# Layer 1 of a two-layer transformer block, worked in two halves of the tokens

## The chip, the cores and the metric

The kernel runs on one core of one Trainium2 chip. The metric is the device time of one execution in microseconds, the median of several runs. The engines are TensorE (PE, with its weight loads listed apart as PEld), VectorE (DVE), ScalarE (ACT), GpSimd (POOL) and SyncE (SP), which issues most of the transfers. Each engine runs its own queue of instructions in order, and engines wait for one another by semaphores.

## The reference

Two transformer layers over 1024 tokens of width 512, all in fp32. Each layer has six modulation vectors, `mod = silu(c) @ wmod`: shift, scale and gate for the attention and for the feed-forward. Cut to what matters here:

```python
for l in range(2):
    sa, ca, ga, sb, cb, gb = mod[l]          # each of width 512
    ga, gb = sign(ga) * max(|ga|, 0.25), sign(gb) * max(|gb|, 0.25)
    x = x + ga * attn[l](layernorm(x) * (1 + ca) + sa)
    x = ... ffn[l](layernorm(x) * (1 + cb) + sb) ...

# layer 0: attention, 32 heads of 128, 8 key heads, causal, 4-bit weights;
#          feed-forward silu(gate) * up -> down, hidden width 1376, each with a LoRA term of rank 16
# layer 1 attention: qkv = h @ w_qkv.T + b_qkv; 32 heads of 16, 8 key heads (each shared by 4)
#          rope on interleaved pairs; causal softmax; out @ w_o.T + b_o
# layer 1 feed-forward: base = h @ base_W.T
#          logits = h @ gate_W.T (28 experts), top 2, softmax of the two
#          lora = sum_e gate_e * 2 * (h @ A_e.T) @ B_e.T, rank 8 each
#          out = x + gb * (base + lora)
```

Layer 1's queries of tokens 0 to 511 need only keys of tokens 0 to 511. Those of 512 to 1023 need all keys.

## The kernel before

Tokens lie on the 128 partitions in 8 tiles; `x[t]` stays in SBUF from start to end. A matmul with a 512-wide fp32 right side appears as two records of about 0.43 us. A product over the width 512 is four matmuls over chunks `c` of 128, with the transposed activations `hT` (features on partitions) as weights.

**Helpers.** `mod_column` (L121) gets a shift or scale by a DVE product and sum over a streamed piece of `wmod` (L127). `mod_gate` (L133) gets a gate vector, replicated over all partitions, by four matmuls (L140), each with a streamed 256 KB piece `wm` (L139). `layernorm_mod` (L153) does statistics on DVE (L160, L161), a square root on ACT (L163), the normalized `xn` (L168), transposes on PE (L176) and the scaled and shifted `hT` on DVE (L184) or ACT (L179). `evict` (L74) takes PSUM to SBUF on DVE or ACT in turn.

**Order.** The code lists the work in order; a tile framework puts in the semaphores and may move an instruction a little ahead or back on its engine. [...] Pools of tiles are opened and closed by stage, and a new stage's tile waits until the old owner of its place has been read for the last time.

1. Layer 0 attention (L196 to L440), untouched but for helpers.
2. Layer 0 feed-forward (L442 to L536). The LoRA terms are merged into the weights by small matmuls and DVE adds (`merge_gate_up` L476, `merge_down` L488). For each of 11 hidden blocks `j` and each half `b` of the tokens, gate and up products (L510), a sigmoid on ACT and two DVE products. Then the down projection: for each of 8 token tiles eleven 512-wide matmuls (L530), the gate (L535) and the add to `x` (L536).
3. Preparation of layer 1's attention (L539 to L648): loads, layernorm of all 8 tiles, modulation chunks 2 to 5, the output bias times its gate added to `x` on POOL (L587), and then in each token tile `t` the qkv product (L606, widths 512 and 256), the bias (L610), rope over separate even and odd elements shared by DVE and POOL (L627, L633, L634), 16 transposes (L646) of queries and of keys repeated four times, and their eviction to `qT1` and `kT1`.
4. Layer 1 attention (L649 to L845) in 16 units of 512 queries (half `Q`) and one key head `g` (four query heads). A unit has three parts: `maxima_steps` (scores of queries on partitions, L682, with row maxima on DVE, L687 and L694), whose result is written into a spare row of the queries (`maxima_rows`, L709 to L714); `probs_steps` (scores again with keys on partitions, L726, a causal mask L733, exp on ACT L737); and `context` (L749), with a copy (L758) and `normalize` (L760). These score matmuls use 32 rows of the array. The maxima of unit n+2 run between the probability steps of unit n; `later(n, fn)` and `tick` place the other parts so many steps behind. After the last unit of a half, `finish_half` transposes the context (L779, L781) and multiplies it by `w_o` (L787, L791, L792). Score tiles take turns in three pairs of PSUM banks; one bank serves contexts and products ("mm"), one transposes ("tr").
5. Layer 1 feed-forward (L847 to L939): loads, layernorm, logits and LoRA-A products (L873), the top-2 routing in small DVE instructions over all 8 tiles (L880 to L913), and in each tile a gated hidden (L917), two transposes (L925, L926), two ACT copies (L928, L929), four base matmuls (L933), two LoRA-B matmuls (L934, L935), the gate (L937), the residual (L938), and the transfer out (L939).

Of the kernel before, what the change touches and what calls it, by code (L numbers as in the profile page):

```python
# [16 lines left out]
P = 128  # L17
# [24 lines left out]
def block_kernel(ctx: ExitStack, tc: tile.TileContext, a: dict, out: bass.AP):  # L42
# [90 lines left out]
    def mod_gate(l, j):  # L133

        rep = mod[l, "rep"]
        ps = psum_mm()
        for k in range(NC):
            wm = tmps["w"].tile([P, D], F32, tag="ws", name="wm")
            nc.sync.dma_start(wm, a[f"wmod{l}"][bass.ts(k, P), bass.ts(j, D)])  # L139
            nc.tensor.matmul(ps, lhsT=rep[:, k, :], rhs=wm, start=(k == 0), stop=(k == NC - 1))  # L140
        sgn = tmp("sgn")
        nc.vector.tensor_scalar(sgn, ps, 0.0, 2.0, ALU.is_ge, ALU.mult)
        nc.vector.tensor_scalar(sgn, sgn, -1.0, None, ALU.add)
        mag = tmp("mag")
        nc.vector.tensor_mul(mag, ps, sgn)
        g = const.tile([P, D], F32, tag=f"gate{j}", name=f"gate{j}")
        nc.vector.scalar_tensor_tensor(g, mag, 0.25, sgn, ALU.max, ALU.mult)
        mod[l, j] = g
# [293 lines left out]
    with ExitStack() as st:  # L442
        hp = st.enter_context(tc.tile_pool(name="f0h", bufs=1))
        wk = st.enter_context(tc.tile_pool(name="f0k", bufs=3))
        tmp_open(st, "f0", wm=4)
        psum_open(st, "psF0")
        sp = st.enter_context(tc.tile_pool(name="f0s", bufs=2, space=PSUM))
# [6 lines left out]
        gu = hp.tile([P, NF, 2, NC, P], F32, tag="gu", name="gu")  # L454
# [8 lines left out]
        dw = hp.tile([P, NF, D], F32, tag="dw", name="dw")  # L463
        for j in range(NF):
            nc.gpsimd.dma_start(dw[:, j, :], a["d_w"][bass.ts(j, P), :])
# [19 lines left out]
        def merge_down(j):  # L485
# [5 lines left out]
            nc.vector.tensor_tensor(dw[:, j, :], dw[:, j, :], ps, ALU.add)  # L491

        mod_prepare(1)
        mod_chunk(1, 0)
        mod_chunk(1, 1)
        hT = layernorm_mod(hp, mod[0, 3], mod[0, 4])
# [4 lines left out]
        hid = []  # L501
        for j in range(NF):
            hj = hp.tile([P, S], F32, tag=f"hid{j}", name=f"hid{j}")
            hid.append(hj)
            for b in range(2):
                pgu = []
                for m in range(2):
                    ps = sp.tile([P, 512], F32, tag=f"gu{m}", name=f"pgu{m}")
                    for c in range(NC):
                        nc.tensor.matmul(  # L510
                            ps, lhsT=gu[:, j, m, c, :], rhs=hT[b][:, c, :],
# [6 lines left out]
                nc.vector.tensor_mul(hj[:, bass.ts(b, 512)], pgu[1], sg)  # L518
# [5 lines left out]

        for b in range(2):
            for i in range(4):
                t = 4 * b + i
                ps = psum_mm()
                for j in range(NF):
                    nc.tensor.matmul(  # L530
                        ps, lhsT=hid[j][:, bass.ts(t, P)], rhs=dw[:, j, :],
                        start=(j == 0), stop=(j == NF - 1),
                    )
                o = tmp("fo")
                nc.vector.tensor_mul(o, ps, mod[0, 5])  # L535
                nc.vector.tensor_add(x[t], x[t], o)  # L536


    with ExitStack() as st:  # L539
        hp = st.enter_context(tc.tile_pool(name="a1h", bufs=1))  # L540
        prep = st.enter_context(ExitStack())
        SC1 = 1.0 / math.sqrt(HD1)
        NQK = NH + NKV
        HH = HD1 // 2
        MX = HD1


        qT1 = hp.tile([P, NKV, S], F32, tag="qT1", name="qT1")
        kT1 = hp.tile([P, NKV, S], F32, tag="kT1", name="kT1")
        v1 = hp.tile([P, NT, NKV, 32], F32, tag="v1", name="v1")  # L550
        mpad = [hp.tile([P, 4, REP, 32], F32, tag=f"mpad{i}", name=f"mpad{i}") for i in range(2)]
        nc.gpsimd.memset(v1, 0.0)
        nc.gpsimd.memset(v1[:, :, :, MX : MX + 1], 1.0)
        for m in mpad:
            nc.gpsimd.memset(m, 0.0)
        cmaskT = hp.tile([P, P], F32, tag="cmaskT", name="cmaskT")
        nc.gpsimd.memset(cmaskT, 0.0)
        nc.gpsimd.affine_select(
            cmaskT, cmaskT, pattern=[[1, P]], compare_op=ALU.is_ge, fill=NEG, base=0,
            channel_multiplier=-1,  # L560
        )

        cwide = hp.tile([P, 512], F32, tag="cwide", name="cwide")
        nc.gpsimd.memset(cwide[:, : 3 * P], 0.0)
        nc.gpsimd.tensor_copy(cwide[:, 3 * P :], cmask)

        hp = prep.enter_context(tc.tile_pool(name="a1i", bufs=1))
        wk = prep.enter_context(tc.tile_pool(name="a1j", bufs=2))
        tmp_open(prep, "a1", wm=4)
        psum_open(prep, "psP1")  # L570
        wqkv = hp.tile([P, NC, NQKV1], F32, tag="wqkv", name="wqkv")
        for c in range(NC):
            nc.sync.dma_start(wqkv[:, c, :], a["w_qkv"][bass.ts(c, P), :])
        cs = hp.tile([P, NT, 2, HH], F32, tag="cs", name="cs")
        nc.sync.dma_start(cs, a["cs1"])
        bqkv = hp.tile([P, NQKV1], F32, tag="bqkv", name="bqkv")
        nc.sync.dma_start(bqkv, a["b_qkv"].partition_broadcast(P))

        hT = layernorm_mod(hp, mod[1, 0], mod[1, 1])
        for j in (2, 3, 4, 5):  # L580
            mod_chunk(1, j)

        bo = tmp("bo")
        nc.sync.dma_start(bo, a["b_o"].partition_broadcast(P))
        nc.gpsimd.tensor_tensor(bo, bo, mod[1, 2], ALU.mult)
        for t in range(NT):
            nc.gpsimd.tensor_tensor(x[t], x[t], bo, ALU.add)  # L587
# [3 lines left out]
        pads = []  # L591
        for i in range(2):
            qpad = hp.tile([P, NH, 32], F32, tag=f"qpad{i}", name=f"qpad{i}")
            nc.gpsimd.memset(qpad, 0.0)
            pads.append(qpad)
        kpad = hp.tile([P, NKV, REP, 32], F32, tag="kpad", name="kpad")
        nc.gpsimd.memset(kpad, 0.0)
        nc.gpsimd.memset(kpad[:, :, :, MX : MX + 1], 1.0)

        for t in range(NT):  # L600
            qkv = wk.tile([P, NQKV1], F32, tag="qkv", name="qkv")
            for n0 in range(0, NQKV1, 512):
                w = min(512, NQKV1 - n0)
                ps = psum_mm()
                for c in range(NC):
                    nc.tensor.matmul(  # L606
                        ps[:, :w], lhsT=tok(hT, c, t), rhs=wqkv[:, c, n0 : n0 + w],
                        start=(c == 0), stop=(c == NC - 1),
                    )
                nc.vector.tensor_add(qkv[:, n0 : n0 + w], ps[:, :w], bqkv[:, n0 : n0 + w])  # L610
            nc.gpsimd.tensor_copy(
                v1[:, t, :, :HD1],
                qkv[:, NQK * HD1 :].rearrange("p (g e) -> p g e", e=HD1),
            )

            qk = qkv[:, : NQK * HD1].rearrange("p (h i two) -> p h i two", i=HH, two=2)
            cosb = cs[:, t, 0, :].unsqueeze(1).to_broadcast([P, NQK, HH])
            sinb = cs[:, t, 1, :].unsqueeze(1).to_broadcast([P, NQK, HH])
            m = {}
            for name, part, tab, eng in (  # L620
                ("rc", 0, cosb, nc.vector),
                ("is", 1, sinb, nc.gpsimd),
                ("rs", 0, sinb, nc.gpsimd),
                ("ic", 1, cosb, nc.vector),
            ):
                m[name] = wk.tile([P, NQK, HH], F32, tag=f"m{name}", name=f"m{name}", bufs=1)
                eng.tensor_tensor(m[name], qk[:, :, :, part], tab, ALU.mult)  # L627
            qpad = pads[t % 2]
            for half, (u, v, op) in enumerate(
                (("rc", "is", ALU.subtract), ("rs", "ic", ALU.add))  # L630
            ):
                sl = slice(half * HH, (half + 1) * HH)
                nc.vector.tensor_tensor(qpad[:, :, sl], m[u][:, :NH, :], m[v][:, :NH, :], op)  # L633
                nc.gpsimd.tensor_tensor(  # L634
                    kpad[:, :, :, sl],
                    m[u][:, NH:, :].unsqueeze(2).to_broadcast([P, NKV, REP, HH]),
                    m[v][:, NH:, :].unsqueeze(2).to_broadcast([P, NKV, REP, HH]),
                    op,
                )
            qf = qpad.rearrange("p h e -> p (h e)")  # L640
            kf = kpad.rearrange("p g r e -> p (g r e)")
            for src in (qf, kf):
                for g0 in range(0, NKV, 4):
                    ps = psum_tr()
                    for i in range(4):
                        nc.tensor.transpose(ps[:, i, :], src[:, bass.ts(g0 + i, P)], ident)  # L646
                    dst = kT1 if src is kf else qT1
                    evict(dst[:, g0 : g0 + 4, bass.ts(t, P)], ps)  # L648
# [373 lines left out]
```

## Time and profile before

| | |
|---|---|
| median of 3 runs | 2067.97 us (2065.26 to 2074.07) |
| the profiled execution | 2064.12 us, its span 2062.1 us |
| mean granted TensorE clock | 0.961 |
| busy PE / PEld / DVE / ACT / POOL | 1895.3 / 872.4 / 1214.6 / 650.7 / 259.2 us |
| a record of the 512-wide base matmul (L933), mean of the group, ends modelled | 592 ns |
| add of 512 wide from PSUM on DVE (L535) | 0.69 us |
| exp of 128 x 1024 on ACT (L737), in the chain of waits | 1.03 us |
| add of 128 x 512 on POOL (L587) | 1.40 us |
| modulation piece `wm`, 256 KB, issue to landing | 3.5 us |

The page cuts the span into forty slices; a digit is the busy share in tenths, and the clock row is the granted TensorE clock in tenths of full speed:

```profile
PE   5979999999999999999999699998779989989988
PEclk9999999999999999999999799998885889999999
```

Each slice is 51.6 us. Layer 1 begins in slice 27 (counted from 0), and the slices behind it have the lower digits.

### The profile page before, as it was taken

The page shows a single profiled execution, that of the slowest core. Times are in us where ns is not written, and L with a number is a line of the kernel's source. Part 1 is how long each engine was busy: PE and PEld are TensorE (multiplying, and loading weights), DVE is VectorE, ACT ScalarE, POOL GpSimd, SP SyncE. Part 2 cuts the span into 40 slices and gives each one's busy share as a digit, 9 for nine tenths or more (in the row PEclk, how much of TensorE's full clock was granted, in tenths as well). Part 3 has the DMA queues.
Part 4 walks back from the last instruction along what each step waited for, and adds up shares of the span by engine and source line. Part 5 has one row for each costly group of instructions (what it writes and reads, how often), then busy time and mean ns, then how long its engine had stood idle before and what let it go on. Part 6 is the DMA issues. An engine that isn't in the chain of part 4 may idle for free.

```text
span 2062.1 us, 20310 instructions
## 1 busy us (share of the span) xinstructions
PE 1895.3 (92%) x6470; PEld 872.4 (42%) x6470; DVE 1214.6 (59%) x2613; ACT 650.7 (32%) x1174; POOL 259.2 (13%) x233
## 2 busy tenths in 40 slices
PE   5979999999999999999999699998779989989988
PEld 3434454444544445444444344443443333323344
DVE  5666656676566765666755532224566776566433
ACT  2133424434244343343354200000012333344531
POOL 0211111121111211212200100001530000000010
PEclk9999999999999999999999799998885889999999
DMA  5355343444334444343533700002100000000011
GB/s 190 101 117 134 94 115 91 107 122 125 89 109 98 132 110 113 97 107 103 131 88 87 260 14 0 0 0 88 39 21 1 1 1 1 1 1 1 1 40 41
DMA packets 88265, 153.15 MB, mean 74 GB/s; under 512 B 20928, under 2 KB 33856, under 8 KB 88160
## 3 DMA queue, kind: packets, MB, share of 16 engines
q1 hardware_dynamic: 87280, 148.98, 26.6%
q0 software_dynamic: 880, 2.88, 0.4%
q8 instruction: 52, 0.85, 0.2%
q14 instruction: 53, 0.43, 0.1%
HBM read 74.18 MB, written 2.10 MB: 37 GB/s over the span
## 4 chain that ended last, share of the span: by engine, by line
PE 70%; DVE 13%; DMA 6%; ACT 5%; issue 3%; SPq 2%; POOL 1%; DVEq 0%; POOLq 0%; ACTq 0%
PE mm L240 13%; PE mm L370 9%; PE pgu L510 7%; PE sc L326 7%; PE mm L359 7%; PE sc L726 6%; PE mm L530 4%; PE ctx L749 4%; PE sc L682 3%; DMA os<-in_s_o_dram 3%; DVE sm L694 2%; ACT pr L737 2%; SPq L350 2%; PE mm L280 1%; DVE pr L348 1%
## 5 line engine op out<-in xcount | busy, mean ns | idle before, releaser
L336 ACT ACTIVATE pr<-sc,nb 128x1024 f32<-128x1024 f32 (+7 forms) x256 | 187.8, 736 | 374.1 <-DVE nb L333 265.0
L240 PE MATMUL mm<-hT,wf 128*128 128x512 f32 x640 | 283.9, 596 | 6.4 <-ACT wf L257 6.4
L359 PE MATMUL mm<-pT,v 128*128 128x512 f32 x576 | 266.6, 609 | 22.8 <-DMA pT<-pr 22.8
L326 PE MATMUL sc<-kT,qT 128*128 128x512 f32 (+3 forms) x768 | 273.3, 487 | 3.4 <-ACT pr L336 3.4
L370 PE MATMUL mm<-wo,ctxT 128*128 128x512 f32 x512 | 236.1, 599 | 16.8 <-ACT ctxT L365 13.4
L737 ACT ACTIVATE pr<-sc 128x1024 f32<-128x1024 f32 (+1 forms) x192 | 152.8, 810 | 235.5 <-DVE sc L733 169.4
L326 PEld LDWEIGHTS sc<-kT,qT 128*128 128x128 f32 x768 | 139.3, 190 | 153.5 <-issue 127.6
L342 ACT ACTIVATE pr<-pr,rs 128x1024 f32<-128x1024 f32 (+7 forms) x256 | 187.4, 768 | 48.6 <-DVE rs L341 48.4
L726 PE MATMUL sc<-qT,kT 32*128 32x512 f32 (+3 forms) x768 | 179.6, 572 | 22.7 <-ACT pr L737 19.3
L348 DVE STREAM_TRANSPOSE pr<-pr 128x1024 f32<-128x1024 f32 (+7 forms) x256 | 178.1, 747 | 21.3 <-ACT pr L342 16.0
L333 DVE TENSOR_REDUCE nb<-sc 128x1 f32<-128x1024 f32 (+7 forms) x256 | 187.6, 749 | 3.4
L240 PEld LDWEIGHTS mm<-hT,wf 128*128 128x128 f32 x640 | 122.2, 192 | 157.3 <-issue 147.9
L359 PEld LDWEIGHTS mm<-pT,v 128*128 128x128 f32 x576 | 111.1, 196 | 149.6 <-issue 134.8
L682 PE MATMUL sc<-kT,qT 32*128 32x512 f32 (+3 forms) x768 | 159.6, 588 | 14.0 <-ACT pr L737 9.8
L376 POOL TENSOR_TENSOR x<-x,ot 128x512 f32<-128x512 f32 x64 | 81.8, 1278 | 672.3 <-DVE ot L375 568.8
L510 PE MATMUL pgu<-hT,gu 128*128 128x512 f32 x352 | 154.9, 600 | 0.8 <-DVE dw L491 0.8
L370 PEld LDWEIGHTS mm<-wo,ctxT 128*128 128x128 f32 x512 | 94.1, 190 | 132.6 <-issue 94.3
L694 DVE CUSTOM_DVE_ANT_0 sm<-sc,cwide 128x128 f32<-128x128 f32 (+3 forms) x256 | 125.1, 489 | 29.6 <-PE sc L726 8.4
L726 PEld LDWEIGHTS sc<-qT,kT 32*128 32x128 f32 x768 | 60.4, 197 | 139.1 <-ACT pr L737 61.8
L341 DVE RECIPROCAL rs<-rs 128x1 f32<-128x1 f32 x256 | 37.9, 156 | 127.8 <-ACT pr L336 126.4
L250 POOL TENSOR_TENSOR qT<-t,t 128x512 f32<-128x512 f32 x64 | 86.1, 1345 | 180.7 <-DVE t L249 180.7
L510 PEld LDWEIGHTS pgu<-hT,gu 128*128 128x128 f32 x352 | 66.9, 192 | 88.6 <-issue 80.7
(159 smaller groups left out, 1812.5 us busy)
## 6 DMA issues: line engine op xcount, KB each, us to landing
pT<-pr SPq DMA_DIRECT2D x128, 128.0 KB, 2.4
pT<-pr SPq DMA_DIRECT2D x128, 112.0 KB, 2.3
pT<-pr SPq DMA_DIRECT2D x128, 96.0 KB, 2.1
pT<-pr SPq DMA_DIRECT2D x128, 80.0 KB, 2.1
wm<-in_wmodT_dram SPq DMA_DIRECT2D x32, 256.0 KB, 3.5
wi<-in_qw_q_dram SPq DMA_DIRECT2D x32, 256.0 KB, 3.0
ws<-in_s_q_dram SPq DMA_DIRECT2D x32, 256.0 KB, 3.7
oi<-in_qw_o_dram SPq DMA_DIRECT2D x32, 256.0 KB, 2.8
```

The source lines that it names most:

```text
L240: nc.tensor.matmul(ps, lhsT=wf[:, c, :], rhs=hT[half][:, c, :], start=(c == 0), stop=(c == NC - 1),)
L326: nc.tensor.matmul(ps[:, n0 : n0 + w], lhsT=qT[u.g * REP + r][:, bass.ts(u.qi, P)], rhs=kT[u.g][:, n0 : n0 + w], start=True, stop=True,)
L333: nc.vector.tensor_reduce(nb, ps[:, :nk], AX.X, ALU.max, negate=True)
L336: nc.scalar.activation(pr.rearrange("p b k i -> p k b i"), ps[:, :nk].rearrange("p (k b i) -> p k b i", b=NB, i=B), AF.Exp, bias=nb, accum ...
L342: nc.scalar.activation(pr, pr, AF.Copy, scale=rs)
L348: nc.vector.transpose(t, t)
L359: nc.tensor.matmul(ps, lhsT=vv[u.g][:, kj, :], rhs=u.pT[:, :, :, kj, :].rearrange("p a r i -> p r a i"), start=(kj == 0), stop=(kj == u.n ...
L370: nc.tensor.matmul(ps, lhsT=u.ctxT[:, r, :], rhs=wo[u.g][:, r, :], start=(r == 0), stop=(r == REP - 1),)
L510: nc.tensor.matmul(ps, lhsT=gu[:, j, m, c, :], rhs=hT[b][:, c, :], start=(c == 0), stop=(c == NC - 1),)
L682: nc.tensor.matmul(ps[:, j, :w], lhsT=qT1[kp, u.g, bass.ts(qi, P)], rhs=kT1[kp, u.g, n0 : n0 + w], start=True, stop=True,)
L726: nc.tensor.matmul(ps[:, j, :w], lhsT=kT1[kp, u.g, bass.ts(kb, P)], rhs=qT1[kp, u.g, u.Q * QW + q0 : (u.Q + 1) * QW], start=True, stop=True,)
L737: nc.scalar.activation(pr[:, :, :w], ps[:, :, :w], AF.Exp, scale=SC1)
```

## The change

Layer 1 is worked in two halves of 512 tokens. `ln_half` does the layernorm of four tiles, `prep_qkv` and `prep_turn` the preparation of one tile. Those of the first half are listed between the down projections of the second half; those of the second half between the steps of the first attention units; the feed-forward of the first half between the steps of the second half's units, by a list `beside` of pieces, each with the number of step pairs after which it is issued. The second half's feed-forward comes last. Rope is rewritten over tables of full width (cosine repeated, sine with its sign) with all its products on DVE; evictions of preparation go to ACT. Gates and chunks of modulation move: chunk 2's gate behind gate/up block 2, the columns 3 and 4 behind blocks 9 and 10, chunk 5's gate into the attention. The pool "big" lets tiles of the stages take one another's place by tags (gate/up weights, then keys and values; hidden, then queries; down weights, then probabilities; `hT` of layer 0, then of layer 1, then contexts, then `hT` of the feed-forward). The streamed `wm` has two buffers in place of four. All layernorm, qkv, transposes and logits of layer 1 take their PSUM from the same three pairs of banks as the scores; `maxima_rows`, `normalize`, the output projection, the gate of chunk 5 and the feed-forward's turns and outputs share one bank ("tr").

The core of the diff; removed lines that come back indented otherwise, or with only names changed, are left out:

```diff
-    def mod_gate(l, j):
+    def mod_gate(l, j, bank=None):
-        ps = psum_mm()
+        ps = (bank or psum_mm)()
...
-        tmp_open(st, "f0", wm=4)
+    tmp_open(st, "f0", bufs=5, wm=2)
+    dwt = big.tile([P, NF, D], F32, tag="c", name="dw")
...
+    def ln_half(half, shift, scale1, pair):
+        mv = small.tile([P, 4, 2], F32, tag="mv", name="mv")
+        for i in range(4):
+            bs = small.tile([P, 6], F32, tag="bnst", name="bnst")
+            nc.vector.bn_stats(bs, x[4 * half + i])
+            nc.vector.bn_aggr(mv[:, i, :], bs)
+        rstd = small.tile([P, 4], F32, tag="rstd", name="rstd")
+        nc.scalar.activation(rstd, mv[:, :, 1], AF.Sqrt, bias=eps_t)
...
+        h = big.tile([P, NC, 512], F32, tag=f"h{half}", name=f"hT{half}")
+        hTc[half] = h
+        for c0 in range(0, NC, 2):
+            ps = pair()
...
             if j in (0, 1, 4, 5):
                 merge_gate_up(4 if j < 4 else 8, j % 4)
             elif j in (6, 7, 8):
                 for i in range(4 * (j - 6), min(NF, 4 * (j - 5))):
                     merge_down(i)
+            elif j == 2:
+                mod_chunk(1, 2)
+            elif j in (9, 10):
+                mod_chunk(1, j - 6)
...
+    sp = st.enter_context(tc.tile_pool(name="ring", bufs=3, space=PSUM))
...
+    def pair():
+        return sp.tile([P, 2, 512], F32, tag="sc", name="sc")
...
+    def prep_ln(half):
+        ln_half(half, mod[1, 0], mod[1, 1], pair)
+        for i in range(4):
+            t = 4 * half + i
             nc.gpsimd.tensor_tensor(x[t], x[t], bo, ALU.add)
...
+    def prep_qkv(t):
+        qkv = pq.tile([P, NQKV1], F32, tag="qkv", name="qkv")
+        ps = pair()
...
+        nc.vector.tensor_add(qkv, ps.rearrange("p j n -> p (j n)")[:, :NQKV1], bqkv)
+        nc.scalar.copy(
...
+        nc.vector.tensor_tensor(
+            t1, qk, cs[:, t, 0, :].unsqueeze(1).to_broadcast(full), ALU.mult
+        )
+        t2 = pq.tile(full, F32, tag="t2", name="t2")
+        for two in range(2):
+            nc.vector.tensor_tensor(
+                t2[:, :, two::2], qk[:, :, 1 - two :: 2],
+                cs[:, t, 1, two::2].unsqueeze(1).to_broadcast([P, NQK, HD1 // 2]), ALU.mult,
+            )
+        nc.vector.tensor_tensor(qpad[:, :, :HD1], t1[:, :NH, :], t2[:, :NH, :], ALU.add)
+        rep = [P, NKV, REP, HD1]
+        nc.vector.tensor_tensor(
+            kpad[:, :, :, :HD1],
...
+    def prep_turn(t):
...
+            ps = pair()
+            psf = ps.rearrange("p j n -> p (j n)")
+            for g in range(NKV):
+                nc.tensor.transpose(psf[:, bass.ts(g, P)], src[:, bass.ts(g, P)], ident)
+            nc.scalar.copy(dst, psf.rearrange("p (g s) -> p g s", s=P))
+
+    prep_ln(0)
+    for i in range(4):
+        down(4 + i)
+        prep_qkv(i)
+        prep_turn(i)
...
+    def psum_one():
+        return psA[0].tile([P, 512], F32, tag="tr", name="tr")
...
+    def out_transpose(Q, i):
...
+        ps = psum_one()
...
+    def project_out(t, cT):
+        po = psum_one()
...
+    def open_late():
+        prep.close()
...
+        nc.sync.dma_start(wo1, a["w_o"].rearrange("(c p) n -> p c n", p=P))
...
         nc.sync.dma_start(wag, a["e_ag"].rearrange("(c p) n -> p c n", p=P))
...
         nc.sync.dma_start(wb, a["e_base"].rearrange("(c p) n -> p c n", p=P))
...
+    def ffn1_logits(half):
...
+        for i0 in range(0, 4, 2):
+            ps = pair()
...
+    def ffn1_route():
...
+        full = [P, 4, NE]
...
+    def ffn1_turn(t):
...
+        ps = psum_one()
...
+    def ffn1_out(t):
+        hgT, eb = late_pool["hgT", t], late_pool["eb"]
+        po = psum_one()
...
+    def ffn1_pieces(half):
+        yield lambda: ln_half(half, mod[1, 3], mod[1, 4], pair)
+        yield lambda: ffn1_logits(half)
+        yield ffn1_route
+        for i in range(4):
+            yield lambda t=4 * half + i: ffn1_turn(t)
+            yield lambda t=4 * half + i: ffn1_out(t)
...
+    beside = [(2, lambda: prep_ln(1))]
+    for i in range(4):
+        beside.append((4 + 5 * i, lambda t=4 + i: prep_qkv(t)))
+        beside.append((7 + 5 * i, lambda t=4 + i: prep_turn(t)))
+    beside.append((24, open_late))
+    beside.append((25, lambda: mod_gate(1, 5, psum_one)))
+    for i, fn in enumerate(ffn1_pieces(0)):
+        beside.append((48 + 4 * i, fn))
+    count = 0
...
+            count += 1
+            while beside and beside[0][0] <= count:
+                beside.pop(0)[1]()
...
+    for fn in ffn1_pieces(1):
+        fn()
```

A unit of the first half has 4 step pairs and one of the second half 8, so counts 2 to 25 lie in the first seven of the first half's units, and 48 to 88 from the end of the second to the end of the seventh of the second half's.

## Prediction

> **What bounds the kernel now.** I read the busy shares first: PE 1895.3 of 2062.1 us, so only 167 us of the whole span are PE idle, and a change that removes no matmul can win only from that idle time and from time at a low clock. Then I cut the part that the change touches into stages and read the table of stretches:
>
> ```profile
> core 0: us, PE busy (x) PEld busy (x) DVE busy (x) ACT busy (x) POOL busy (x), PEclk, DMA share, GB/s
> 1178.20:1345.50 167.30, 166.53 (x408) 71.11 (x408) 48.17 (x78) 14.42 (x23) 0.00 (x0) 0.99 0.06 23
> 1345.50:1421.20 75.70, 75.54 (x177) 33.09 (x175) 16.80 (x31) 0.30 (x1) 0.05 (x1) 1.00 0.00 0
> 1421.20:1467.90 46.70, 27.35 (x74) 14.55 (x75) 26.75 (x48) 3.30 (x5) 23.05 (x26) 0.75 0.44 139
> 1467.90:1534.00 66.10, 51.24 (x230) 34.90 (x230) 43.24 (x58) 9.38 (x16) 29.75 (x36) 0.95 0.00 0
> 1534.00:1557.00 23.00, 19.03 (x77) 9.31 (x78) 17.50 (x69) 0.25 (x1) 0.00 (x0) 0.56 0.16 47
> 1557.00:1715.00 158.00, 143.87 (x881) 56.16 (x879) 114.46 (x363) 49.35 (x72) 0.00 (x0) 0.81 0.00 1
> 1715.00:1968.00 253.00, 233.56 (x1504) 80.51 (x1504) 144.97 (x348) 115.77 (x142) 5.08 (x4) 1.00 0.00 1
> ...
> 1992.00:2062.10 70.10, 62.76 (x212) 35.02 (x210) 27.48 (x59) 10.88 (x28) 1.27 (x1) 1.00 0.08 30
> ```
>
> In order: gate/up, down projection, the layernorm of layer 1, its eight tiles of preparation, the maxima of two attention units, the eight units of the first half, the eight of the second, and the last feed-forward. Gate/up, down, the second half and the tail are full of PE at full clock. The hole is 1421 to 1534: 112.8 us with 78.6 of PE. The chain of waits says what fills it:
>
> ```profile
> 1434.71 4.95 PE mm L140 x8
> 1439.67 3.33 DMA wm<-in_wmodT_dram
> 1443.76 3.50 DMA wm<-in_wmodT_dram
> 1448.49 3.76 DMA bo<-in_b_o_dram
> 1452.42 1.28 POOL bo L585
> 1453.77 5.98 POOL x L587 x5
> 1459.75 1.03 issue
> 1460.79 3.95 POOL x L587 x3
> 1467.92 1.94 PE tr L646 x8
> ...
> 1480.09 1.74 PE mm L606 x8
> ```
>
> Transfers of the modulation chunks, then POOL's adds of the bias, then in each tile transposes that wait for rope (period 8.8 us, 1486.10 to 1494.90 in the chain).
>
> **Layernorm and half the preparation go beside the down projection.** Before, 1345.5 to 1534 is 188.5 us. Afterwards PE does there: eight down tiles, 75.5; four qkv products, each 3.44 (four 512-wide matmuls, as the chain's "3.44 PE mm L933 x8") plus 1.74 (the row above), 20.7; sixteen transposes a tile, 19.8 us for 128 in the groups of L646, so 2.5, together 10; the layernorm's transposes of one half, half of the 8.1 us of L176's 32, so 4. That is 110. Rope now lies on DVE alone: add 1.1 (L610, twice 557 ns), first product 0.86 (0.69 for 512 elements times 640/512), two strided products at 0.61 (L627 mrc; its twin mic took 1.21, but beside POOL, so I take 0.61), the query's sum 0.69: 3.9 us before the first transpose. The scheduler puts four matmuls of the next down tile (3.44) there, so about 1 us stalls for three tiles; the fourth has no down tile behind it: 4.6 and 1 for the copy. The layernorm chain stands behind six down matmuls (5.2 against about 6), 1 us. Together 117, **-71**. Bounds -60 (rope wholly bare) and -76. The eight POOL adds (11.0 us) and the modulation transfers leave the path: no later wait in the instruction order is for them until an attention result is added to x.
>
> **The modulation work moves into gate/up**, where PE has no idle. One gate of chunk 2 is four matmuls, 3.44; two of them wait for transfers issued only when the first two free their buffers (two buffers now, four before; 3.5 us each), 0 to 1.5, I take 1. Column work (L127, 0.69 each) stands on DVE ahead of the merges that PE needs: 0 to 6, I take 2. The first down tile newly waits for the last gate result, 1.5. **+8**. At the head, the gate/up weights no longer queue behind five modulation transfers on SP, but the merges stand ahead of the second layernorm half on DVE: **-1** (-4 to +3).
>
> **The other half's preparation goes into the units of the first half** (1557 to 1715). PE gains 4 x 7.7 = 30.8, 4 for the layernorm, and the gate of chunk 5: 3.44 and a bare transfer of 3.5, as its second pair of buffers queues on SP behind the late weights. That is 41.7. Against it: idle PE, 14.1 us, of which I give it a third (5), because the three pairs of PSUM banks through which scores and preparation now both go are a queue in order, about 1 us lost per piece (+4); and the clock. The slices of this stage are the odd row:
>
> ```profile
> 1445.00:1450.00 5.00, 1.99 (x3) 0.96 (x4) 2.10 (x6) 0.00 (x0) 0.00 (x0) 0.50 0.77 244
> 1450.00:1455.00 5.00, 5.00 (x12) 2.21 (x11) 1.62 (x2) 0.00 (x0) 2.50 (x3) 0.87 0.24 76
> ```
>
> ```profile
> 1560.00:1570.00 10.00, 9.26 (x44) 3.56 (x40) 4.72 (x17) 3.13 (x4) 0.00 (x0) 0.50 0.01 2
> ```
>
> After the idle at 1440 the clock is half, and 128-row matmuls had it back within the next 5 us. From 1540 to 1595 it stays half for 55 us although PE is 93% busy, with 32-row matmuls. The Trainium skill ("TensorE: Matmul & The Clock Gate", Part 1) says that one window of some 3.4 us of sustained work releases the clock, however many instructions that is; it excepts only transposes (Part 4). By the rule this stage would have been warm already and the change would win nothing from the clock: +41. By the rows a busy PE is not enough and dense qkv products would release it: a half-clock unit takes 21.8 us (context copies at 1578.7 and 1600.5), a full one 15.2 to 16.1 (1616.6, 1631.8), so two units get back 6 each. I take the rows, -12, and with it 41.7 - 5 + 4 - 12, **+28** (+15 to +70). The page's table "Why this matters for your kernels" also speaks against the change's end: no PE gap over about 3 us. The tail below opens such gaps.
>
> **The first half's feed-forward goes into the second half's units**, which are bound by PE: layernorm transposes 2.5 (half of L176's 4.9 there), logits 7.2 (half of L873's 14.4), hidden transposes 2.2, outputs 4 x 5.16: 32.5, less 4 of the 19.4 us idle. **+28** (+20 to +38; the high end if the 7 us of routing, in order on DVE, hold up the masks that exp waits for).
>
> **The tail.** The second out-projection uses one bank for transpose and product: **+3**. The feed-forward of one half, from 70.1: x, statistics, square root and first xn 5.5 with nothing beside; transposes and hT 4.1; logits 7.8; routing 7 (from 2013.61 to 2020.4 in the chain, covered before by base products on the second bank, 4.91 busy of 5 us at 2015; bare now); first turn 1; four outputs at 5.16 + 0.3 x 2 + 0.28 x 2 + 0.69 = 7, as a turn must wait for the last output to leave its bank, 28; the last result and its transfer 4; 2 for the clock after the bare gap. 59, **-11** (-18 to -5).
>
> **Sum.** -1 + 8 - 71 + 1 (maxima) + 28 + 28 + 3 - 11 = -15. On the profiled execution (2064.12, 2.0 around its span) 2049; the median shown is 3.9 above that execution. I give **2049**: the profile's sum, as single runs scatter as far as those 3.9.
>
> **Rivals.**
> - *The idle takes it all in* (0.2). Preparation fills all 14.1 us of idle (+15), the feed-forward sinks in at +20, down hides rope at -76, tail -13: 2020. For it: PE idle in these stages is waiting for ACT's exp and DVE's mask, and independent matmuls could stand there. Against: the queue is in order, and pieces come every fourth or fifth step, not where a gap is.
> - *In series, not beside* (0.22, the slower side). Place: the shared ring of three bank pairs. While a piece holds a pair until DVE or ACT has read it, scores have two, and PE stands behind it. Then each prepared tile costs product 5.2, rope 4.5, transposes 2.5, two copies 2: 14.2 x 4 = 57, layernorm 5, gate 7: +69, and feed-forward +38: 2100. For it: DVE is busy 114.46 of 158 already, and gets 18 more. Against: three pairs suffice for scores and maxima now, with PE at 143.87 of 158. It makes the kernel slower once both attention stages together grow by over 75 us (56 in my sum).
> - *The clock stays half* (0.06). All eight units at 21.8 us (+16) and preparation at half speed (some 60): 2100.
> - *A draw* (0.14): half the ring's price, 2060 to 2078. The change does what it says in the instruction order of each engine; that it doesn't overlap as meant is the second rival.
>
> **Numbers.** My forecast has 0.38 (2035 to 2057). What can't be told from no change is 0.5%, 10 us either side of 2068. Faster: 0.38 and 0.2, less a little of the high edge: 0.56. Same 0.17, slower 0.27. The range reaches from the first rival's better half to the slow rivals: 2012 to 2096; the likeliest case's own is 2032 to 2064.
>
> **What would show it.** Right: no stretch after the down projection with over 4 us of idle PE but the last rope; clock 1.0 from the first qkv product in the units of the first half; that stage 180 to 190 long, the next about 280; a bare routing of 7 us in the tail. Wrong: PE waiting in those stages for reads of the bank pairs, or a half clock past the third unit, means the slow side; first-half units with preparation under 19 us each mean the fast one.

## The result, and the profile after

The changed kernel takes 2073.55 us (median of 20 runs, 2061.22 to 2082.36), the kernel before 2067.64 (20 runs beside it). The ratio is 1.0031, interval 1.0016 to 1.0046: a little slower, where 2049 was forecast. The profiled execution lies at the slow edge: 2082.02 us, span 2080.2, 18.1 above the span of before. So the stages below hold 12 us that the medians don't; where they come from is part of the answer.

The table of stretches of the changed kernel, with the columns of the one before: gate/up; down with the first half's preparation; the maxima of two units; the first half's units; the second half's units; all behind them. The bounds are the same events as before: the maxima are given 23.0 us in every kernel, so that their row measures nothing of its own, and the units end 3.3 us ahead of the eighth context copy and 1.7 ahead of the last.

```profile
core 0: us, PE busy (x) PEld busy (x) DVE busy (x) ACT busy (x) POOL busy (x), PEclk, DMA share, GB/s
1178.90:1350.90 172.00, 171.05 (x416) 72.66 (x414) 59.32 (x108) 14.57 (x24) 1.05 (x4) 0.98 0.13 40
1350.90:1466.60 115.70, 107.83 (x324) 55.31 (x324) 45.10 (x69) 10.02 (x15) 17.57 (x16) 0.98 0.06 21
1466.60:1489.60 23.00, 19.68 (x82) 9.38 (x84) 17.31 (x69) 3.32 (x3) 0.00 (x0) 0.57 0.00 1
1489.60:1695.40 205.80, 186.92 (x1030) 81.66 (x1030) 132.17 (x393) 57.43 (x84) 0.15 (x1) 0.84 0.05 17
1695.40:1996.50 301.10, 279.12 (x1608) 101.16 (x1608) 158.48 (x385) 120.11 (x155) 5.09 (x4) 0.94 0.01 4
1996.50:2080.20 83.70, 57.42 (x176) 27.76 (x174) 22.59 (x54) 11.35 (x24) 5.06 (x4) 0.91 0.03 13
```

| stage | before | after | moved | forecast |
|---|---|---|---|---|
| head and gate/up (1153.3 to the first down tile) | 192.2 | 197.6 | +5.4 | +7 |
| down to the first maxima | 188.5 | 115.7 | -72.8 | -71 |
| maxima | 23.0 | 23.0 | 0 | +1 |
| first half's units | 158.0 | 205.8 | +47.8 | +28 |
| second half's units | 253.0 | 301.1 | +48.1 | +28 |
| behind them | 94.1 | 83.7 | -10.4 | -8 |
| sum | | | +18.1 | -15 |

The gain came (-72.8 where -71 was forecast), and then two stages gave it back. PE's busy time says how: it rose by 43.1 us in the first half's units and by 45.6 in the second's. What grew is for the most part not PE waiting. Adding up the idle times that the timeline shows on PE, the first stage waits 18.2 us (13.2 before), the second 22.2 (19.6).

The table of stretches cut to five microseconds a row, four rows out of the second half's units of the changed kernel:

```profile
1735.00:1740.00 5.00, 2.77 (x24) 1.20 (x24) 3.83 (x12) 1.35 (x3) 0.96 (x1) 1.00 0.00 0
1740.00:1745.00 5.00, 5.00 (x23) 1.65 (x20) 2.38 (x3) 2.04 (x3) 0.00 (x0) 0.58 0.00 0
...
1775.00:1780.00 5.00, 5.00 (x22) 1.25 (x22) 1.33 (x2) 1.02 (x1) 0.00 (x0) 0.50 0.00 0
...
1830.00:1835.00 5.00, 5.00 (x24) 1.64 (x24) 2.00 (x6) 0.83 (x2) 0.00 (x0) 0.50 0.00 0
```

A stretch with PE little over half busy (2.77 of 5), and after it PE is fully busy at a clock of 0.58; at 1775 and again at 1830 it is fully busy at half clock. These are the three places at which the clock falls in this stage. In the profiled execution of before, the stage was at 1.00 throughout.

What stands ahead of the first place and of the third, from the timelines of PE, DVE and ACT in order of time:

```profile
1735.99 0.69 DVE L455 BATCH_NORM_STATS2 bnst<-x 128x6 f32<-128x512 f32 x1 [1.38 <-POOL x L894]
1738.07 1.13 PE L827 MATMUL sc<-q,kv 32*128 32x512 f32 x4 [1.76 <-DVE mx L794]
...
1820.71 0.59 PE L827 MATMUL sc<-q,kv 32*128 32x512 f32 x2
1822.12 0.28 DVE L957 TENSOR_TENSOR oh<-rank,first 128x112 f32<-128x112 f32 x1
1822.31 0.43 DVE L833 TENSOR_TENSOR sc<-sc,cmaskT 128x256 f32<-128x256 f32 x1
1822.83 1.02 ACT L838 ACTIVATE pspace<-sc 128x1024 f32<-128x1024 f32 x1 [1.97 <-DVE sc L833]
1823.91 1.13 PE L827 MATMUL sc<-q,kv 32*128 32x512 f32 x4 [1.75 <-ACT pspace L838]
```

At 1735 a statistic of the feed-forward's layernorm waits on DVE for POOL's add to `x`, and the row maxima behind it in DVE's queue hold up PE. At 1821 the scores are ready, but steps of the routing stand on DVE ahead of the mask (L833), the exp waits for the mask, and PE for the exp.

Two rows of PE's timeline near the end: the first turn after the bare routing, and the second, which waits for the last output to leave the one bank:

```profile
2044.28 0.47 PE L990 MATMUL tr<-ident,hg 128*128 128x128 f32 x1 [5.85 <-DVE hg L982]
...
2054.60 0.33 PE L990 MATMUL tr<-ident,hg 128*128 128x128 f32 x1 [0.78 <-DVE eo L1007]
```

### The profile page after: what moved, and what is told of

Same layout as the page of the kernel before. It is cut to its first block, busy times and chain, and to the rows that moved or that the text cites. A ratio compares the mean times of both kernels' runs of the same rounds, so it can differ in the third digit from the quotient of the medians.

```text
span 2080.2 us, 20215 instructions
## 1 busy us (share of the span) xinstructions
PE 1925.2 (93%) x6470; PEld 878.4 (42%) x6470; DVE 1198.8 (58%) x2612; ACT 659.9 (32%) x1183; POOL 224.6 (11%) x192
## 4 chain that ended last, share of the span: by engine, by line
PE 69%; DVE 15%; ACT 5%; DMA 5%; issue 3%; SPq 3%; POOL 1%; DVEq 0%; POOLq 0%; ACTq 0%
PE mm L240 12%; PE mm L370 8%; PE pgu L580 7%; PE sc L326 7%; PE mm L359 7%; PE sc L827 6%; PE ctx L850 4%; PE mm L611 3%; PE sc L783 3%; DMA os<-in_s_o_dram 3%; SPq L350 2%; PE sc L684 2%; DVE pr L348 2%; DVE q L794 2%; DVE nb L333 2%
## 5 line engine op out<-in xcount | busy, mean ns | idle before, releaser
L370 PE MATMUL mm<-wo,ctxT 128*128 128x512 f32 x512 | 236.1, 599 | 16.6 <-ACT ctxT L365 13.4
L827 PE MATMUL sc<-q,kv 32*128 32x512 f32 (+3 forms) x768 | 184.0, 590 | 26.9 <-ACT pspace L838 18.6
L838 ACT ACTIVATE pspace<-sc 128x1024 f32<-128x1024 f32 (+3 forms) x160 | 127.7, 811 | 236.4 <-DVE sc L833 167.3
L342 ACT ACTIVATE pr<-pr,rs 128x1024 f32<-128x1024 f32 (+7 forms) x256 | 187.4, 768 | 47.8 <-DVE rs L341 47.6
L783 PE MATMUL sc<-kv,q 32*128 32x512 f32 (+3 forms) x768 | 166.6, 600 | 13.3 <-ACT pspace L838 7.7
L370 PEld LDWEIGHTS mm<-wo,ctxT 128*128 128x128 f32 x512 | 94.1, 190 | 132.4 <-issue 93.8
L794 DVE CUSTOM_DVE_ANT_0 q<-sc,cwide 128x128 f32<-128x128 f32 (+3 forms) x256 | 125.2, 489 | 32.1 <-PE sc L783 11.1
L827 PEld LDWEIGHTS sc<-q,kv 32*128 32x128 f32 x768 | 60.9, 200 | 138.3 <-ACT pspace L838 59.6
```

What stands on the lines that cost most here:

```text
L342: nc.scalar.activation(pr, pr, AF.Copy, scale=rs)
L370: nc.tensor.matmul(ps, lhsT=u.ctxT[:, r, :], rhs=wo[u.g][:, r, :], start=(r == 0), stop=(r == REP - 1),)
L783: nc.tensor.matmul(ps[:, j, :w], lhsT=u.q[kp, bass.ts(i, P)], rhs=kT1[kp, u.g, n0 : n0 + w], start=True, stop=True,)
L794: nc.vector.tensor_tensor_reduce(u.space(2)[:, :w], ps[:, j, :w], cwide[:, 512 - w :], 1.0, -3e38, ALU.add, ALU.max, accum_out=u.mx[:, i, ...
L827: nc.tensor.matmul(ps[:, j, :w], lhsT=kT1[kp, u.g, bass.ts(kb, P)], rhs=u.q[kp, q0:QW], start=True, stop=True,)
```

## The experiments

The theory: the stages of the units pay for every piece in full, since PE is their bound, and the clock takes its own share. The rivals: the pieces are hidden but badly placed; the shared bank pairs make the units wait; the dense products help the clock; the lower clock is chance.

**The last feed-forward on other banks.** In `ffn1_turn` and `ffn1_out`:

```diff
-        ps = psum_one()
+        ps = pair()[:, 0, :] if t >= 4 else psum_one()
...
-        po = psum_one()
+        po = pair()[:, 0, :] if t >= 4 else psum_one()
```

> Only the last half's feed-forward changes: its turns and outputs take their bank from the three pairs, which nothing else uses by then. If the tail is long because a turn waits for the last output to leave the one bank (outputs every 7.2 us, where five matmul groups of 5.2 are worked), the period falls to about 5.4 and the tail, 59.7 us in the trace of the changed kernel, to 53 to 55: 5 to 7 us faster than the changed kernel's 2073.5. If the bank was hidden and the period is PE's own, nothing moves (under 1 us in the tail).

2067.51 us (12 runs), ratio to before 1.0000 (0.9975 to 1.0024): 6 us less than the changed kernel, as expected. The stretch behind the units fell from 83.7 to 75.7 us. The outputs now follow one another every 5.4 us, where the one bank gave 7.2. The second half's units and the stretch behind them:

```profile
1693.00:1989.60 296.60, 273.89 (x1608) 100.22 (x1608) 158.16 (x385) 119.90 (x155) 5.09 (x4) 0.96 0.01 4
1989.60:2065.30 75.70, 53.74 (x176) 27.50 (x174) 22.41 (x54) 11.37 (x24) 5.06 (x4) 0.93 0.04 14
```

**The first half's feed-forward behind the attention.** Both halves' pieces come last, on the three pairs of banks, the second half's logits and routing kept in the space of the probabilities so that the two halves don't wait for each other's buffers.

```diff
-    for i, fn in enumerate(ffn1_pieces(0)):
-        beside.append((48 + 4 * i, fn))
...
-    for fn in ffn1_pieces(1):
+    first, second = list(ffn1_pieces(0)), list(ffn1_pieces(1))
+    for fn in first[:2] + second[:1] + first[2:3] + second[1:2] + first[3:] + second[2:]:
         fn()
```

> No feed-forward beside the second half's attention units; both halves' feed-forward come after them, with turns and outputs in the three pairs of banks. My theory (a PE-bound stage pays for every piece in full, and the pieces also let the clock drop, 36 us at half clock): the second half's stage falls from 301 back to 250 to 256 us at clock 1.00, the stages behind it grow from 83.7 to 90 to 96; in all some 38 us less, 2035. Rival (pieces stand beside the attention and only their placing is a bit clumsy, 15 us of loss): the stages behind grow by 45 for PE's 32 and the bare chains, and the kernel gets no faster, 2070 to 2085. Rival (the slower clock of that stage comes by chance or from a hot chip, not from the pieces): it stays near 0.94 and the stage at 265 to 270.

2055.69 us (19 runs), ratio 0.9949 (0.9933 to 0.9966). Its two last stretches, the second half's units and all behind:

```profile
1690.40:1951.50 261.10, 239.10 (x1508) 82.18 (x1512) 144.53 (x348) 115.98 (x143) 5.08 (x4) 0.97 0.00 1
1951.50:2050.90 99.40, 84.23 (x276) 44.23 (x268) 36.35 (x90) 15.62 (x36) 5.29 (x4) 0.97 0.06 22
```

Against the kernel with only the banks changed (296.6 and 75.7 us) the units lose 35.5 and the end gains 23.7: 11.8 in all, and the medians say the same, 2067.51 to 2055.69. The tail takes a whole half's feed-forward, for which PE is busy 30.5 us longer (53.74 to 84.23), in 23.7. I read this as one half's work standing where the routing and layernorm of the other left PE idle; the clock there also rose, from 0.93 to 0.97. In the units next to nothing was hidden. I had expected twice the gain (2035). I had taken the stage at 250 to 256 us and clock 1.00; it came at 261.1 and 0.97 with no product of the feed-forward in it, between my theory and the rival of chance (265 to 270). The layernorm's statistics still stand there: the framework moved them ahead, between the units.

**The second half's preparation ahead of the attention.**

```diff
-    beside = [(2, lambda: prep_ln(1))]
-    for i in range(4):
-        beside.append((4 + 5 * i, lambda t=4 + i: prep_qkv(t)))
-        beside.append((7 + 5 * i, lambda t=4 + i: prep_turn(t)))
-    beside.append((24, open_late))
+    beside = [(24, open_late)]
...
+    prep_ln(1)
+    nxt = prep_mm(4)
+    for i in range(4, 8):
+        ps, nxt = nxt, prep_mm(i + 1) if i < 7 else None
+        prep_rope(i, ps)
+        prep_turn(i)
     psd.close()
```

(`prep_mm` and `prep_rope` are `prep_qkv` cut in two, so that one tile's product can stand ahead of another's transposes.)

> The second half's preparation is done before the attention, tile after tile, with the product of tile i+1 ahead of the transposes of tile i; nothing but the gate of chunk 5 stays beside the first half's units. The stage before grows by 4 x 7.7 of PE, 4.6 for the last rope and 5 for layernorm: 40 to 45. My theory (beside the units the preparation costs its PE time in full, and it doesn't raise the clock): the first half's units fall from 206 to 160 to 168 us with a clock of about 0.8 as before, and the sum is even within 5 us. Rival (dense products do raise the clock there, and without them it is lower): the units stay over 172 and the kernel is 8 us or more slower. Rival (the three pairs of banks are what the units wait for when preparation holds them): the units fall under 158 and the kernel is 8 us or more faster.

2063.62 us (12 runs), ratio 0.9982 (0.9962 to 1.0003). Down with all eight tiles' preparation, the maxima, and both halves' units:

```profile
1351.80:1499.70 147.90, 138.09 (x464) 76.67 (x464) 62.07 (x95) 20.06 (x29) 17.55 (x16) 0.98 0.05 16
1499.70:1522.70 23.00, 19.44 (x85) 9.19 (x84) 17.58 (x69) 3.48 (x4) 0.15 (x1) 0.64 0.35 125
1522.70:1682.40 159.70, 144.34 (x886) 55.94 (x881) 116.29 (x367) 47.24 (x70) 0.00 (x0) 0.84 0.01 4
1682.40:1975.40 293.00, 270.43 (x1608) 98.00 (x1608) 158.39 (x385) 120.21 (x155) 5.08 (x4) 0.98 0.01 4
```

I had expected the sum to be even within 5 us; the kernel came out 9.9 us faster in the medians, as the rival of the bank pairs had it, but with the units at 159.7 us and not under 158. Four tiles and a layernorm take 32.2 us alone (115.7 to 147.9; I had said 40 to 45) and 46.1 beside the units (205.8 to 159.7). At a mean clock of 0.84 in both rows, the longer stage also loses some 7 us more to the clock (205.8 x 0.16 against 159.7 x 0.16), and the experiment with twice the dense work shows that this part varies as much without any pieces. So "beside" is dearer than "after one another" by 14 us in the two traces, and by 10 in the medians, which are the better figure. Done alone, a product runs under each tile's rope and the clock is 0.98. Which part of the 10 us is due to that, and which to the shared bank pairs, no run separates.

**Both.**

> Both of the last two edits: only the first half's layernorm and preparation beside the down projection is left of the overlap. My theory: the two effects add, about 2035 (-38 and 0). If what the pieces cost is shared between stages (a clock state carried on from the first half's units into the second), the two together give more than the sum, under 2025.

2046.29 us (4 runs), ratio 0.9897 (0.9858 to 0.9936). From the changed kernel's 2073.55 us the two edits alone took 17.9 and 9.9 us, together 27.3: they add. My 2035 was too low for the same reason as above.

**Twice the dense work.** In `prep_qkv` of the changed kernel:

```diff
-        for j in range(2):
+        for j in [0, 1] * (1 + t // 4):
```

> The changed kernel with one edit: the qkv products of the second half's four tiles, beside the first half's units, are each worked twice (the second pass overwrites the first with the same values), 4 x 5.2 = 20.7 us more of dense 128-row matmuls and nothing else. If dense products release the clock there, as my prediction had it, the twofold dose costs clearly less than its own length: the stage's clock rises from 0.84 to over 0.90 and the stage, 206 us, grows by under 10. If the clock is set by the units' own 32-row matmuls and the pieces are paid in full, the clock stays within 0.82 to 0.88 and the stage grows by 19 to 25, the kernel to 2092 to 2098.

2095.85 us (4 runs), ratio 1.0167 (1.0134 to 1.0199). The first half's units:

```profile
1490.10:1714.80 224.70, 204.53 (x1094) 93.01 (x1094) 131.66 (x393) 57.47 (x84) 0.15 (x1) 0.87 0.05 16
```

The stage took 18.9 us more for 20.7 us of dense products, at a clock of 0.87, about as the second expectation had it. With the single dose, four profiled executions of this stage had 0.83, 0.84, 0.86 and 0.87; with no preparation in it, six had 0.81 (before), 0.84, 0.79, 0.78, 0.85 and 0.82. That looks like 0.03 of clock won, but a mean clock rises by itself when full-clock work is added to a stage. The time lost to the clock is length x (1 - clock): 26 to 35 us in the four with a single dose, 29 with the double one, and 23 to 36 in the six without. The dense products won back nothing that shows.

**Without the base matmuls** of the first half's output tiles:

```diff
-        for c in range(NC):
+        for c in range(NC if t >= 4 else 0):
...
-        nc.tensor.matmul(po, lhsT=hgT[:, 0, :], rhs=eb[0], start=False, stop=False)
+        nc.tensor.matmul(po, lhsT=hgT[:, 0, :], rhs=eb[0], start=(t < 4), stop=False)
```

This kernel leaves the base products out of the first half's output.

> The changed kernel without the four base matmuls of each of the first half's four output tiles (their products are left out of the output): 4 x 3.44 = 13.8 us less of PE beside the second half's units; every DVE and ACT step, wait and bank stays. If that stage pays for PE's time in full, it falls from 301 by 13 to 20 us (the upper end if longer pieces also cost clock), and the kernel by as much. If what it pays for is the interruption, DVE's in-order steps or the shared bank, it falls by under 7.

2058.71 us (12 runs), ratio 0.9976 (0.9953 to 1.0000), so 0.55% under the changed kernel's ratio, 11 us for 13.8 us of products. The second half's units:

```profile
1694.40:1973.60 279.20, 256.69 (x1576) 91.87 (x1576) 158.42 (x385) 120.08 (x155) 5.08 (x4) 0.98 0.01 5
```

The kernel with preparation ahead has the same stage whole at the same clock, 293.0 us at 0.98: 13.8 us longer. That this is the forecast figure to the tenth is luck, since 0.01 of clock is 3 us here. Against all four traces with the whole stage, at equal clock (below), it is 11 us. So these products are paid for nearly one for one. This run doesn't price the interruptions, the DVE steps and the bank, which stayed.

**A version that keeps the part that paid.** From "both": the gate of chunk 5 goes into the gap of the last bare rope, the second out-projection to the pairs, and the first half's layernorm and logits between the out-projections.

```diff
+        if i == 3:
+            mod_gate(1, 5)
         prep_turn(i)
...
-        po = psum_one()
+        po = pair()[:, 0, :] if t >= 4 else psum_one()
...
     while late:
         tick()
+        ticks += 1
+        if ticks == 10:
+            first[0]()
+        if ticks == 13:
+            first[1]()
```

> The earlier kernel with both halves' feed-forward and the preparation taken out of the units (2046.3), and three more edits: the gate of chunk 5 stands in the gap of the last rope of the first half, in place of the first half's units; the second out-projection writes to the three pairs of banks, so that a transpose doesn't wait for the last product to be read; and the first half's layernorm and logits stand between those transposes and products. From its trace: 6.2 us of bare rope can take the gate's 3.4 and its transfer; the out-projections have a period of 5.9 at 4.4 of PE[...]. I expect 6 to 7 us off the units' stage and 6 to 9 off the stages behind: 2031 to 2036. If those gaps were hidden by something later, or the clock alone rules, it stays at 2042 to 2047.

2043.41 us (4 runs), ratio 0.9905 (0.9869 to 0.9942), where I had expected 2031 to 2036. It was measured on another chip than "both", with single runs from 2035.44 at clock 0.965 to 2048.25 at 0.957. That didn't tell it from "both", so the two were measured again on one chip.

> The lean kernel again, on one chip with the next one, since their first runs were on two chips and the clock differs from execution to execution. From the two traces at equal clock (2035.4 at 0.965 against 2044.4 at 0.964) I expect it 6 to 8 us under the next one and 1.2 to 1.5% under the kernel before. If the gaps that it closes were worth nothing, both are equal within 3 us.

> The kernel with the feed-forward and the preparation taken out of the units, again: 0.9 to 1.1% under the kernel before.

2037.65 us (4 runs), ratio 0.9868 (0.9839 to 0.9898), against 2046.14 (4 runs), ratio 0.9903 (0.9881 to 0.9925): 8.5 us better in the medians. The two intervals overlap, but each of its four runs is faster than each of the other's. Down with preparation and gate, the first half's units, and all behind the attention in the lean kernel's repeated run:

```profile
1349.40:1501.10 151.70, 143.26 (x475) 77.53 (x474) 63.24 (x99) 19.96 (x29) 17.21 (x16) 0.98 0.06 19
...
1524.10:1678.10 154.00, 138.85 (x878) 54.19 (x878) 113.84 (x363) 47.11 (x71) 0.00 (x0) 0.85 0.00 1
...
1942.70:2035.50 92.80, 81.47 (x276) 45.01 (x268) 34.52 (x86) 15.54 (x36) 5.06 (x4) 0.95 0.06 23
```

The end is 92.8 us where "both" has 99.4; the gate costs 3.5 in its new place (148.2 to 151.7), where the rope gap hid less of it than I thought. It beats the kernel before by 1.3%.

## Why the prediction was wrong, point by point

**Right: where the gain is and how large.** The stretch from the down projection to the first maxima was to take 117 us and took 115.7. The uncovered rope of the fourth tile is where it was put: the timeline of PE shows

```profile
1451.47 5.32 PE L684 MATMUL sc<-wqkv,hT 128*128 128x512 f32 x16
1462.97 1.94 PE L727 MATMUL sc<-ident,qpad 128*128 128x128 f32 x8 [6.18 <-DVE qpad L706]
```

6.2 us against 5.6 in the sum; part of it is the four `xn` of the second half, which the framework put ahead of that rope on DVE. The three covered ropes stalled PE by 0.17 us each, not 1. Head and gate/up (+7, measured +5.4) and the tail (-8, -10.4) were right within 3 us.

**Wrong: the price of the preparation beside the first half's units.** The sum was 41.7 us of PE and transfer, less 5 for idle taken in, plus 4 for the bank pairs, less 12 for the clock: +28. Measured: +47.8. The two discounts are the step that failed; neither came. Idle on PE was not filled but rose by 5 us. The clock gave nothing back: as the section on twice the dense work shows, the time lost to it is the same with the pieces and without. Once it is taken out, what is left is length x clock, the time that the stage would take at full clock if all of it stretches with the clock. That is 173 to 175 us with the pieces and 128 in the trace of before. The difference, about 46, is the sum without its two discounts. I had read two full-clock units and two half-clock units in one trace, and a recovery in the dense stage at 1450, and concluded that dense products among 32-row ones would hold the clock up.

I had also read that trace too coarsely. It was not at half clock for 55 us from 1540 to 1595, and the 93% belongs to 1560 to 1595 alone. Two rows cut it finer:

```profile
1570.00:1580.00 10.00, 9.02 (x59) 3.45 (x57) 6.34 (x25) 2.87 (x5) 0.00 (x0) 0.67 0.00 0
1580.00:1595.00 15.00, 14.41 (x67) 5.75 (x67) 7.50 (x25) 3.84 (x5) 0.00 (x0) 0.51 0.01 2
```

At 1574 the clock was full for about 3 us, with nothing but the units' own work on PE, and then half again. What came and went without dense products was no sign that dense products would bring it.

**Mis-sized: the feed-forward beside the second half's units.** The sum was 32.5 us of PE less 4 of idle: +28. Measured: +48.1 in the traces. With the pieces, this stage took 301.1, 296.6, 296.6 and 293.0 us at clocks of 0.94, 0.96, 0.96 and 0.98 (changed kernel, tail banks, twice dense, preparation ahead). Without, it took 264.6, 260.8, 260.8, 261.1, 256.6 and 253.0 at 0.96, 0.97, 0.97, 0.97, 0.99 and 1.00 (the two lean runs, "both" again, feed-forward behind, "both", and before). Length x clock is 283 to 287 in the first group and 253 to 254 in the second: 31 us, so next to nothing of the 32.5 was hidden. The other 17 of the 48.1 are time lost to the clock, a term that the sum put at nothing. It has three parts.

- Behind the routing the clock falls in all five traces that have it in this stage (the four and the one without base products), after 4 us in which PE was busy for 2.2 to 2.8, and stays at half for 3.4 to 10.2 us. In the six others it stays full from there to the end of the stage. So this piece does cost clock, 2 to 5 us. The forecast named the way in its high end, routing in order on DVE that holds up the masks, but its sum left it out.
- Some 40 and 70 us into the stage, beside the first half's out-projection, the clock falls one to three times in all ten traces of changed kernels, with the feed-forward's products or without; before lost nothing there. This usually costs 5 to 7 us. So it doesn't come from the feed-forward's products. What opens the gap no run isolates, and there is one trace of before.
- In the changed kernel's profiled execution the second of these falls lasted 20 us, where nine others lasted 3.4. That is a chance of this execution.

**The sum at the medians.** The profiles differ by 18.1 us, the medians by 5.9, so the forecast of -15 missed the medians by 21. In the mean of the four traces with the pieces of each stage (204.4 and 296.8 us), the first half's units are 18 over the forecast and the second half's 16. The other parts went 7 better, and before's median is 3.5 above its profiled execution. That makes 24 for 21, which is as near as single traces come.

**The rivals.** "A draw" (2060 to 2078) holds the measured time, but by luck: it got there with half the price of the bank pairs. "In series, not beside" had the outcome: the two stages of the units grew by 96 us together, over its 75. Its place is not shown to be the cause. Waits on PE grew by only 5.0 and 2.6 us, and work is in series mainly because PE was the bound. "The clock stays half" was right that nothing would come back from the clock; half clock past the third unit, at 1611 to 1625, is the sign that was named for the slow side. But no more time was lost to it in that stage than without the pieces. "The idle takes it all in" fell. What the forecast knew (a change that removes no matmul can win only from PE's idle time or low clock) it counted as won without a gap in which the work would stand.

## What to carry to other kernels

- Moving work beside a stage in which PE is 91% busy is moving it into a queue. Price it at its full PE time, and count a discount for idle only if the piece stands in the gap itself; here 74 us of pieces left 33 us of idle unfilled. The same piece in a chain with bare latency (routing, layernorm, rope) was partly free: 30.5 us of PE in 23.7 in the tail, some of it by a better clock.
- Look also at a piece's small steps on the other engines. The routing stood on DVE ahead of a mask, PE waited 1.75 us, and half clock followed.
- Cut such a change by its parts before judging it. The 73 us of the down stage are not all gain, since half of the preparation only moved elsewhere; with all eight tiles in it the stage takes 147.9 us, 41 under before. Taking the pieces out of the units gave 0.9897 of the time before, and three more edits 0.9868.
- Compare stages by length x clock and by length x (1 - clock), each apart. Otherwise a chance of the clock reads as a cost of the change, and a longer stage as a better clock.

## What the runs showed of the hardware

One program varies by 21 us from execution to execution, and the clock goes with most of it. Over the 20 runs of the changed kernel the span and the granted clock have a correlation of -0.92: the fastest took 2061.22 us at 0.964, the slowest 2082.36 at 0.954. A line through the 20 gives 16.6 us for a hundredth of clock, where a hundredth of a 2070 us span is 20.7: most of the lost clock is paid for. In the stages that the tables cut, the largest spread is in the attention units: the clock of the first half's units was between 0.78 and 0.87 over all kernels, that of down and gate/up between 0.97 and 1.00.

In all eleven traces the granted clock is either full or half, and each stretch at half clock inside the span is a multiple of 3.4 us, from one to eleven of them. (Rows of one microsecond show it.)

As to the rule of the Trainium skill that the prediction weighed ("TensorE: Matmul & The Clock Gate", Part 1: one busy window of about 3.4 us releases the clock): the runs agree with the length of the window and not with the one. Many stretches of half clock ended after a single one, but PE was busy for 5.00 of 5 us at 0.50 (1775 above) in a stretch of six, and for 14.41 of 15 us at 0.51 (1580 to 1595 before). Added dense products of 20.7 us did not shorten such stretches in sum. The same page's table "Why this matters for your kernels", which the prediction also weighed, warns of PE gaps over about 3 us. Here the clock fell after single gaps of 1.75 us and 1.19 us with matmuls between them. What holds the clock down among 32-row matmuls was not found.
